# Cross attention on one core: from mixing the values with the attention to mixing x and applying the value weights behind it

## The chip, the core and the metric

The kernel runs on one core of a Trainium2 chip. The core has engines that work side by side, each through its own list in order: PE (matmuls, with PEld for the weight loads that overlap them), DVE (vector work), ACT (activations and copies), POOL (vector work on SBUF, and the issue of accumulating DMAs) and SP (here only issues DMAs). PE writes PSUM, eight banks of 512 columns; DVE and ACT read PSUM, POOL does not. The metric is the device time of one execution in microseconds.

## The reference

For each of 32 batches, with x and y of 256 channels x 1024 positions in fp32:

```python
x_q = jnp.einsum('oc,bcn->bno', w_qk, y)
x_k = jnp.einsum('oc,bcn->bon', w_qk, x)
x_v = jnp.einsum('oc,bcn->bon', w_v, x) + b_v[None, :, None]
energy = jnp.einsum('bnc,bcm->bnm', x_q, x_k)
attention = jax.nn.softmax(energy, axis=-1)
attention = attention / (1e-07 + attention.sum(axis=1, keepdims=True))
x_r = jnp.einsum('bcn,bnm->bcm', x_v, attention)
x_r = jax.nn.relu(jnp.einsum('oc,bcn->bon', w_t, x - x_r) + b_t[None, :, None])
return x + x_r
```

## The kernel before

Batches are worked through one after another, 1024 positions as eight row tiles n of 128, 256 channels as two halves. The weights are folded once at the start: `gw` is w_qk with itself, so that the energies are y times (gw x); `vw` is w_t times w_v; `tw` is w_t. Both folded ones carry a factor of 4096 (`UP`), which the next step takes out.

**Three forms.** Every operand of a large matmul is kept as three tiles, called HIGH, REST and LOW (`FORMS`), and every product is three matmuls, one for each form. Whoever makes an operand therefore makes three: a rounded copy (ACT), and two that come out of a difference and a sum (DVE from PSUM, POOL from SBUF, or an accumulating DMA that POOL issues).

**One batch.** Its matmuls, all of 128 x 128 weights, are:

- keys (k): `xf,gw`, 24 matmuls of 512 columns, into a pair of PSUM banks; ACT, DVE, DVE make the three forms `gf` of it.
- values (V): `vw,xf`, 48 matmuls of 256 columns: eight position tiles, each with x as the weights and `vw` as the moving operand, so that the result stands with positions on the partitions. ACT and DVE make its three forms, `uf`.
- straight (X): `xf,tw`, 24 of 512 columns; ACT adds the bias and puts it into `xe`.
- energies (E): `gf,yf`, for each row tile n 12 of 512 columns, into one of two pairs of banks that alternate. Then DVE takes the row minimum (`nm`), ACT the exponential with the row sum (`rs`), DVE its reciprocal (`ri`), ACT the HIGH form `ef` (two halves, h), DVE the REST form (r) and the column sums `acc` (sum), ACT a scaled copy (s), POOL the LOW form (l). When h, r and sum have read a half of the pair, the energies of tile n+2 may be written there.
- attention (A): `ef,uf`, for each n 12 of 512 columns, summed over all n into the last two pairs of banks, one pair for each half of the channels.

Behind the last A stands the end of the batch: DVE turns `acc` into the inverse column sums `rc` and divides (`z`), POOL adds `xe` (join), ACT takes the relu, POOL adds `xo`, which is x loaded a second time, and SP stores.

The queries y come by one load for the HIGH form and a second read of the same half batch that is accumulated onto the negated HIGH form, issued by POOL (`rest`, lines 176-177).

**The order.** `InOrder` (lines 55-69) ties every instruction of PE, DVE, ACT and POOL behind the last one written for that engine, so that the order of the code is the order of each engine; plain loads and stores on SP are placed by the framework that builds the program. The loop over batches (lines 605-752) writes the order by hand; the last batch has a table of words of its own, `STEPS` (lines 812-823), one word for each step, which stands in the code in one list for all engines.

Of the kernel before, what the change touches and what calls it, by code (L numbers as in the profile page):

```python
# [17 lines left out]
def kernel(  # L18
# [34 lines left out]
    sp = ctx.enter_context(tc.tile_pool(name="sp", bufs=4))  # L53
# [76 lines left out]
    xbias = const.tile([P, KC, 1], F32, name="xbias")  # L130
    for _ in range(5):
        pe.matmul(banks[:, 7, :P], zeros, zeros, start=True, stop=True)
    make_identity(nc, ident)

    work = one.tile([P, 4, KC * C], F32, tag="xe", name="work")

    def area(j):
        return work[:, j].rearrange("p (k c) -> p k c", k=KC)
# [22 lines left out]

    class Queries:

        def __init__(self, q):
            self.b, self.half = divmod(q, MH)
            self.from_ = raw(f"y_{self.b}_{self.half}").rearrange("p (k n) -> p k n", k=KC)
            load(self.from_, y_half(self.b, self.half))

        def high(self):
            self.f = yp.tile([P, FORMS, KC, MB], F32R, tag="yf", name=f"yf_{self.b}_{self.half}")  # L170
            act.copy(self.f[:, HIGH], self.from_)
# [32 lines left out]
    class Batch:  # L204

        def __init__(self, b):
            self.b = b
            self.at = b % 2
            self.row, self.ef, self.uf = {}, {}, []

        def load_x(self):
            self.xr = [raw_x("x", self.b, k) for k in range(KC)]
# [17 lines left out]
        def channels(self, p, w, i):  # L230

            for h in range(MH):
# [10 lines left out]
        def keys(self, i):  # L243
            if i == 0:
                self.gf = one.tile([P, FORMS, KC, N], F32R, tag="gf", name=f"gf_{self.b}")
            p = pair((self.at + i) % 2)
            self.channels(p, gw.forms, i)
            return Right(p, [self.gf[:, j, i] for j in range(FORMS)])

        def first_keys(self, j, k):  # L250
# [12 lines left out]
            return [Right(pair(i), [self.gf[:, f, i] for f in range(FORMS)]) for i in range(KC)]  # L263
# [17 lines left out]
        def straight(self, c, to=3):  # L281
            self.channels(pair(to), tw, c)
            self.x_from = pair(to)

        def straight_out(self, c, halves=None):
            if not hasattr(self, "xe"):
                self.xe = one.tile([P, KC, N], F32, tag="xe", name=f"xe_{self.b}")
            at = slice(0, MH) if halves is None else halves
            act.activation(
                self.xe[:, c].rearrange("p (h m) -> p h m", h=MH)[:, at],  # L290
                self.x_from[:, at],
                AF.Identity,
                bias=xbias[:, c],
                scale=1.0,
# [5 lines left out]
        def energy(self, n, halves=range(MH)):  # L300
            p = self.place(n)
            yf = ys[self.b * MH + n // HT].f
            for h in halves:
                for j in ORDER:
                    for k in range(KC):
                        matmul(
                            p[:, h],
                            yf[:, j, k, ts(n % HT, P)],
# [32 lines left out]
        def scaled(self, n):  # L341
            act.mul(self.ef[n][:, LOW], value(self.ef[n][:, HIGH]), 1.0 / UP)

        def low(self, n, at=slice(0, None)):
            f = self.ef[n][:, :, at]
            pool.tensor_tensor(f[:, LOW], value(f[:, LOW]), value(f[:, REST]), ALU.add)
# [44 lines left out]
        def inverse(self):  # L391
# [11 lines left out]
            self.turned()  # L403

        def turned(self):
# [11 lines left out]
        def divided(self, c):  # L417
            if c == 0:
                self.z = one.tile([P, KC, N], F32, tag="z", name=f"z_{self.b}")
            dve.scalar_tensor_tensor(  # L420
                self.z[:, c], flat(pair(2 + c)), ubias[:, c], self.rc, ALU.add, ALU.mult
            )

        def joined(self, c):
            pool.tensor_tensor(self.z[:, c], self.z[:, c], self.xe[:, c], ALU.add)

        def relu(self, c):
            act.activation(self.z[:, c], self.z[:, c], AF.Relu)
# [7 lines left out]

        def end_sum(self, c, at=slice(0, None)):
            xo = self.xo[c][:, at]
            pool.tensor_tensor(xo, xo, self.xe[:, c, at], ALU.add)

        def end_least(self, c, at=slice(0, None)):
            act.mul(self.xe[:, c, at], self.xe[:, c, at], -1.0)
# [23 lines left out]
        def piece(self, c, h):  # L466
# [3 lines left out]
            return pair(2 + c)[:, h], self.z[:, c, at], self.xe[:, c, at], self.xo[c][:, at]  # L470
# [74 lines left out]
    corner = work[:, 3, :P]  # L545
# [30 lines left out]
    def biases():  # L576
# [4 lines left out]
        for k in range(KC):  # L581
            act.activation(
                xbias[:, k], wtb[:, k : k + 1], AF.Identity, bias=bt[:, k], scale=-1.0
            )

    y0 = ys[0]
    y0.high()
    k0, k1 = cur.first_keys(LOW, 1)
    pool.tensor_tensor(y0.f[:, REST], y0.from_, value(y0.f[:, HIGH]), ALU.subtract)
    k1.high()  # L590
    k1.low()
    k0.high()
    k1.rest()
    k0.low()
    k0.rest()
    y0.scaled()
    pool.tensor_tensor(y0.f[:, LOW], value(y0.f[:, LOW]), value(y0.f[:, REST]), ALU.add)
    tw = const.tile([P, FORMS, KC, C], F32R, name="tw")
    th, tl, td = (tw[:, j].rearrange("p k c -> p (k c)") for j in range(FORMS))
    wd = work[:, 2]  # L600
    ys[2] = Queries(2)

    first_order = [(1, 0), (1, 1), (0, 0), (0, 1)]
    last = None
    for b in range(B - 1):
        nxt = Batch(b + 1)

        if b == 0:
            v0 = cur.values(0)
            v0.high()  # L610
            v1 = cur.values(1)
            v0.low()
            v0.rest()
            act.copy(th, wtT)
            pool.tensor_tensor(wd, wtT, value(th), ALU.subtract)
            pool.tensor_tensor(
                product, wt, bv.unsqueeze(1).to_broadcast([P, KC, C]), ALU.mult
            )
            ys[1].high()
            v1.high()  # L620
            act.mul(tl, wd, UP)
            pool.tensor_tensor(td, wtT, value(tl), ALU.subtract)
            cur.energy(0)
            cur.lowest(0)
            v1.low()
            ys[1].minus()
            ys[1].rest()
            biases()
            cur.exp(0)
            cur.energy(1)  # L630
            cur.recip(0)
            v1.rest()
            cur.forms(0)
            ys[1].scaled()
            ys[1].low()
            cur.lowest(1)
            cur.share(0)
            cur.straight(0)
            cur.exp(1)
            cur.straight_out(0)  # L640
            cur.recip(1)
            cur.straight(1, 2)
            for h in range(MH):
                cur.high(1, h)
                cur.rest(1, h)
            cur.straight_out(1)
            cur.scaled(1)
            cur.low(1)
        else:
            v0 = cur.values(0)  # L650
            v0.high()
            v1 = cur.values(1)
            v0.low()
            v0.rest()
            cur.energy(0)
            v1.high()
            v1.low()
            cur.lowest(0)
            v1.rest()
            cur.straight(0)  # L660
            cur.exp(0)
            cur.recip(0)
            cur.high(0, 0)
            cur.rest(0, 0)
            cur.high(0, 1)
            cur.rest(0, 1)
            cur.straight_out(0)
            cur.scaled(0)
            cur.low(0)
            cur.energy(1)  # L670
            cur.lowest(1)
            cur.share(0)
            cur.exp(1)
            cur.recip(1)
            cur.straight(1, 2)
            last.load_out()
            for h in range(MH):
                cur.high(1, h)
                cur.rest(1, h)
            cur.straight_out(1)  # L680
            cur.scaled(1)
            cur.low(1)
            last.relu(0)
            last.put(0)
        nxt.load_x()
        cur.energy(2)
        cur.share(1)
        for n in range(2, NT):
            if n > 2:
                cur.energy(n)  # L690
            cur.lowest(n)
            if n > 2:
                cur.share(n - 1)
            cur.exp(n)
            cur.recip(n)
            cur.forms(n)
            cur.attention(n - 2, first_order if n == 2 else None)
            if b == 0 and n == 4:
                gather_groups()
            if n == 2:  # L700
                nxt.x_high(0)
                nxt.x_rest(0)
            elif n == 3:
                nxt.x_high(1)
                nxt.x_rest(1)
                nxt.x_scaled(0)
            elif n == 4:
                nxt.x_scaled(1)
                nxt.x_low(0)
                nxt.x_low(1)  # L710
            if last and n == 5:
                last.relu(1)
                last.put(1)
            elif n == 5:
                ys[2].high()
                ys[2].minus()
                ys[2].rest()
            elif n == 6 and not last:
                ys[2].scaled()
                ys[2].low()  # L720
        k0 = nxt.keys(0)
        cur.share(NT - 1)
        k0.high()
        k0.low()
        k0.rest()
        cur.columns()
        cur.inverse()
# [129 lines left out]
```

## Time and profile before

| | |
|---|---|
| median of 3 runs | 1941.99 us (1941.97 to 1942.38) |
| the profiled execution | 1942.1 us, of which its span is 1940.3 us |
| granted clock of PE | 0.999 |
| PE busy | 1934.2 us, 9249 matmuls |
| DVE, ACT, POOL busy | 1558.5, 1463.5, 1261.3 us |
| DMA | 235.35 MB, 81852 packets |

The span is the time from the first to the last instruction of the profiled execution; the device time has 1.8 us more around it. PE counts as busy while a matmul is in flight, so neighbours overlap: the duration of one (389 ns) is its latency, and the rate is read from the distance of starts in the timeline. Almost every instruction stands under the one line of the helper that records them (line 66), so the groups are told apart by the names of their tiles. In a row `xf<-x` the tile on the left is written and the one on the right read.

### The profile page before, as it was taken

Reading aid. Unit: us, or ns where it says so; the run is one execution under the profiler, and the core shown is the slowest. Engines: PE = TensorE matmul, PEld = TensorE weight load, DVE = VectorE, ACT = ScalarE, POOL = GpSimd, SP = SyncE. Lnnn points to the kernel's source line nnn. Section 1 sums busy time; section 2 is a strip of 40 time slices with the busy share of each in tenths; the row PEclk is TensorE's granted clock in tenths of the full one; section 3 lists DMA queues with packets and bytes.
Section 4 is the critical chain, followed back from the end, with each engine's and each line's share of the span. In section 5 each row is a group of like instructions: output and inputs, shape, how many; then the busy total and the mean of one; then the engine's idle time right before and its main releaser. Section 6 shows DMA issues by size and latency. Waiting matters only on the chain.

```text
span 1940.3 us, 25180 instructions
## 1 busy us (share of the span) xinstructions
PE 1934.2 (100%) x9249; PEld 1632.4 (84%) x9249; DVE 1558.5 (80%) x2153; ACT 1463.5 (75%) x1874; POOL 1261.3 (65%) x654
## 2 busy tenths in 40 slices
PE   9999999999999999999999999999999999999998
PEld 8888888888888888888888888888888888888887
DVE  7887788877888778887788887888877888778888
ACT  7778777787777877778777778777777777877776
POOL 5576766667656676566766666665766657666566
PEclk9999999999999999999999999999999999999999
DMA  4654545545456444554445554545545455454541
GB/s 139 131 137 116 124 112 120 146 115 130 110 112 149 118 122 109 123 138 121 118 117 123 130 127 112 124 116 130 131 119 120 120 120 134 116 121 118 120 120 44
DMA packets 81852, 235.35 MB, mean 121 GB/s; under 512 B 7488, under 2 KB 8384, under 8 KB 81728
## 3 DMA queue, kind: packets, MB, share of 16 engines
q0 software_dynamic: 35136, 98.58, 29.1%
q1 hardware_dynamic: 46176, 134.76, 20.4%
q8 instruction: 73, 1.20, 0.3%
q14 instruction: 51, 0.42, 0.1%
q10 hardware_dynamic: 416, 0.39, 0.1%
HBM read 134.61 MB, written 33.55 MB: 87 GB/s over the span
## 4 chain that ended last, share of the span: by engine, by line
PE 100%; DMA 0%; DVE 0%; issue 0%
PE banks L66 100%; DMA stage<-in_L_xattn_w_qk_dram 0%; DVE banks L66 0%; DVE z L66 0%
## 5 line engine op out<-in xcount | busy, mean ns | idle before, releaser
L66 POOL TENSOR_TENSOR ef<-ef 128x1024 fp32r<-128x1024 f32 x253 | 608.9, 2407 | 450.2 <-ACT ef L66 443.3
L66 PE MATMUL banks<-gf,yf 128*128 128x512 f32 x3072 | 739.0, 389 | 0.0
L66 PE MATMUL banks<-ef,uf 128*128 128x512 f32 x3036 | 730.3, 389 | 0.0
L66 PEld LDWEIGHTS banks<-gf,yf 128*128 128x128 f32 x3072 | 574.5, 188 | 118.1 <-issue 0.3
L66 PEld LDWEIGHTS banks<-ef,uf 128*128 128x128 f32 x3036 | 569.9, 188 | 118.1
L66 DVE SCALAR_TENSOR_TENSOR ef<-banks,ri,ef 128x512 fp32r<-128x512 f32 x506 | 356.8, 747 | 204.2 <-ACT ef L66 204.2
L66 ACT ACTIVATE banks<-banks,nm 128x1024 f32<-128x1024 f32 x256 | 278.0, 1086 | 216.3 <-DVE nm L66 214.3
L66 DVE TENSOR_REDUCE nm<-banks 128x1 f32<-128x1024 f32 x256 | 313.0, 1222 | 86.5 <-PE banks L66 86.5
L66 ACT ACTIVATE ef<-banks,ri 128x512 fp32r<-128x512 f32 x506 | 320.7, 685 | 69.1 <-DVE ri L66 67.7
L66 DVE SCALAR_TENSOR_TENSOR acc<-banks,ri,acc 128x512 f32<-128x512 f32 x448 | 314.1, 743 | 0.2
L66 ACT ACTIVATE ef<-ef 128x1024 fp32r<-128x1024 f32 x253 | 268.9, 1063 | 5.9
L66 POOL DMA_DIRECT2D yf<-in_ctx_dram x63 | 77.1, 1223 | 188.7 <-ACT yf L66 186.6
L66 PEld LDWEIGHTS banks<-vw,xf 128*128 128x128 f32 x1536 | 188.7, 192 | 2.6
L66 PE MATMUL banks<-vw,xf 128*128 128x256 f32 x1536 | 189.5, 283 | 0.0
L66 PE MATMUL banks<-xf,gw 128*128 128x512 f32 x768 | 184.8, 389 | 0.0
L66 PE MATMUL banks<-xf,tw 128*128 128x512 f32 x768 | 184.3, 389 | 0.0
L66 PEld LDWEIGHTS banks<-xf,tw 128*128 128x128 f32 x768 | 144.2, 188 | 29.9
L66 PEld LDWEIGHTS banks<-xf,gw 128*128 128x128 f32 x768 | 144.1, 188 | 29.9
L66 POOL TENSOR_TENSOR z<-z,xe 128x1024 f32<-128x1024 f32 (+1 forms) x63 | 163.7, 2815 | 4.8 <-DVE z L66 4.8
L66 POOL TENSOR_TENSOR z<-z,xo 128x1024 f32<-128x1024 f32 (+1 forms) x65 | 152.9, 2353 | 0.2 <-DVE z L66 0.2
L66 POOL TENSOR_TENSOR xf<-x,xf 128x1024 fp32r<-128x1024 f32 x62 | 149.5, 2412 | 0.0
L66 ACT ACTIVATE yf<-yf 128x1024 fp32r<-128x1024 f32 x127 | 131.1, 1055 | 2.0
(89 smaller groups left out, 1336.8 us busy)
## 6 DMA issues: line engine op xcount, KB each, us to landing
x<-in_x_dram SPq DMA_DIRECT2D x64, 512.0 KB, 3.5
y<-in_ctx_dram SPq DMA_DIRECT2D x64, 512.0 KB, 4.6
xo<-in_x_dram SPq DMA_DIRECT2D x64, 512.0 KB, 3.6
yf<-in_ctx_dram POOLq DMA_DIRECT2D x63, 512.0 KB, 6.5
yf<-yf POOLq DMA_DIRECT2D x63, 512.0 KB, 5.3
xf<-xf POOLq DMA_DIRECT2D x62, 512.0 KB, 6.3
out_dram<-z SPq DMA_DIRECT2D x62, 512.0 KB, 2.9
out_dram<-z SPq DMA_DIRECT2D x4, 256.0 KB, 2.0
```

What stands on the lines that cost most here:

```text
L66: self.last = getattr(self.engine, name)(*args, **kwargs)
```

## The change

In all batches but the first and the last (`late(b)`) the order of the two products is turned round: the attention is applied to x itself, and `vw` to the result.

- The values matmuls go (48 of 256 columns). `uf` is now made from x with positions on the partitions. For that x is loaded another time, as 32-row groups (`load_positions`, eight DMAs of 128 KB to a batch, pieces of 512 bytes), DVE transposes it in place in blocks of 32 x 32 (`turned_x`, tt), and ACT and POOL make three forms of it: th (ACT copy), tm (POOL subtract), tl (ACT scale), tr (POOL add). `turned` reads the loaded tile in runs of 32 elements.
- The blocks bring the positions into another order, and the row tiles of y are formed in that order: `ordered` and `loaded` let the y steps write or read in runs of 32. REST of y is now a subtraction on POOL (yr) instead of the second, accumulated read.
- A sums the mixed x. Behind the last A three forms of it are made from PSUM: zh (ACT copy), zr and zl (DVE), for each half of the channels. Then `mixed` (W): `vw` as the weights, the mixed x as the moving operand, 24 matmuls of 512 columns. It writes the pair of the other half (`pair(3 - c)`), and the division reads that.
- The output: the addition of x on POOL with its load `xo` is replaced by an accumulating DMA from x into `z` (add), and the store is a step of its own (st).
- The two nested orders of before become three tables of words: `FIRST` (batches 0 and 1), `STEADY` (batches 2 to 30, one pass each) and a new `STEPS`. A leading `+` means the batch after, `-` the one before. E, X, k and W are now halves of 6 matmuls, A halves of 3, which other steps stand between.
- Pools: `xe` gets a pool of three buffers, one for each half of the channels; `sp` has three instead of four. The four buffers of raw loads now also hold the two tiles of turned x.

The places at the seam of two batches, as the two built programs have them (before: batches 10 and 11; `ef_11_0` is row tile 0 of batch 11). PE before:

```order
L66 MATMUL banks_76<-ef_10_6_5344,uf_10_1_5059 128x512 x12
L66 MATMUL banks_76<-xf_11_5195,gw_113 128x512 x12
L66 MATMUL banks_76<-ef_10_7_5383,uf_10_1_5059 128x512 x12
L66 MATMUL banks_76<-vw_148,xf_11_5195 128x256 x48
L66 MATMUL banks_76<-gf_11_5402,yf_11_0_4983 128x512 x12
L66 MATMUL banks_76<-xf_11_5195,tw_179 128x512 x12
L66 MATMUL banks_76<-gf_11_5402,yf_11_0_4983 128x512 x12
```

PE of the changed kernel at the same seam, up to the first two matmuls of W (`zf` is the mixed x):

```order
L67 MATMUL banks_79<-ef_10_6_5279,uf_10_1_4928 128x512 x9
L67 MATMUL banks_79<-ef_10_7_5305,uf_10_1_4928 128x512 x12
L67 MATMUL banks_79<-xf_11_5082,tw_176 128x512 x12
L67 MATMUL banks_79<-gf_11_5355,yf_11_0_4905 128x512 x24
L67 MATMUL banks_79<-zf_10_0_5400,vw_154 128x512
L67 MATMUL banks_79<-zf_10_1_5406,vw_154 128x512
```

The values are gone from the seam; between the last attention of batch 10 and the W that needs it stand half of the straight product and two row tiles of energies of batch 11, and behind the 24 matmuls of W come the other half, two more tiles of energies, and then the first attention of batch 11.

DVE of the changed kernel at that seam (`nm_11_0` is the row minimum of tile 0, `rc` the inverse column sums, `z` the division):

```order
L67 SCALAR_TENSOR_TENSOR gf_11_5355<-banks_79,gf_11_5355 128x1024
L67 TENSOR_TENSOR zf_10_0_5400<-banks_79,zf_10_0_5400 128x1024
L67 SCALAR_TENSOR_TENSOR zf_10_1_5406<-zf_10_1_5406,banks_79 128x1024
L67 SCALAR_TENSOR_TENSOR zf_10_0_5400<-zf_10_0_5400,banks_79 128x1024
L67 TENSOR_TENSOR zf_10_1_5406<-banks_79,zf_10_1_5406 128x1024
L67 TENSOR_REDUCE nm_11_0_5458<-banks_79 128x1
L67 STREAM_TRANSPOSE rc_10_5463<-sc_92 128x1024
L67 TENSOR_REDUCE nm_11_1_5465<-banks_79 128x1
L67 RECIPROCAL ri_11_0_5476<-rs_11_0_5461 128x1
L67 SCALAR_TENSOR_TENSOR z_10_5484<-banks_79,ubias_up_95,rc_10_5463 128x1024
L67 SCALAR_TENSOR_TENSOR ef_11_0_5479<-banks_79,ri_11_0_5476,ef_11_0_5479 128x512 x2
```

The four forms of the mixed x stand where the forms of the values stood, and the first division now stands in the middle of the first two row tiles of the next batch.

POOL before, at the seam:

```order
L66 TENSOR_TENSOR ef_10_7_5383<-ef_10_7_5383 128x1024
L66 DMA yf_11_1_5456<-in_ctx_2048_dram 128x2x512
L66 DMA yf_12_0_5464<-in_ctx_2048_dram 128x2x512
L66 TENSOR_TENSOR z_10_5481<-z_10_5481,xe_10_5100 128x1024 x2
L66 DMA yf_11_1_5456<-yf_11_1_5456 128x1024
L66 DMA yf_12_0_5464<-yf_12_0_5464 128x1024
L66 TENSOR_TENSOR ef_11_0_5576<-ef_11_0_5576 128x1024
```

and in the changed kernel:

```order
L67 TENSOR_TENSOR ef_10_7_5305<-ef_10_7_5305 128x1024
L67 DMA z_9_5010<-in_x_dram 128x1024
L67 TENSOR_TENSOR yf_11_1_5229<-y_11_1_5203,yf_11_1_5229 128x8x4x32
L67 DMA yf_11_1_5229<-yf_11_1_5229 128x1024
L67 TENSOR_TENSOR uf_11_1_5402<-xp_11_1_5208,uf_11_1_5402 128x1024
L67 TENSOR_TENSOR uf_11_0_5260<-xp_11_0_5108,uf_11_0_5260 128x1024
L67 TENSOR_TENSOR yf_12_0_5379<-y_12_0_5206,yf_12_0_5379 128x8x4x32
L67 DMA yf_12_0_5379<-yf_12_0_5379 128x1024
L67 TENSOR_TENSOR uf_11_1_5402<-xp_11_1_5208,uf_11_1_5402 128x1024
L67 TENSOR_TENSOR z_10_5484<-z_10_5484,xe_10_0_4948 128x1024
L67 TENSOR_TENSOR ef_11_0_5479<-ef_11_0_5479 128x1024
```

Five subtractions and additions in runs of 32 now stand between the last LOW form of one batch and the first of the next, and one join instead of two.

SP in the changed kernel, from the stores of batch 10 on:

```order
L539 DMA out_0_dram<-z_10_5484 128x1024
L114 DMA x_13_0_5982<-in_x_dram 128x1024
L539 DMA out_0_dram<-z_10_5484 128x1024
L114 DMA x_13_1_6008<-in_x_dram 128x1024
L265 DMA xp_13_0_6056<-in_x_dram 32x8x128 x4
L180 DMA y_13_1_6151<-in_ctx_2048_dram 128x2x512
L180 DMA y_14_0_6154<-in_ctx_2048_dram 128x2x512
L265 DMA xp_13_1_6156<-in_x_dram 32x8x128 x4
```

The second store of a batch now stands behind a load of x for a later batch, which waits until POOL has read the raw buffer that it takes; before, one store stood between the two loads of `xo` and the other behind the loads of x.

The diff, cut to its core:

```diff
+    xep = ctx.enter_context(tc.tile_pool(name="xep", bufs=3))
+    sp = ctx.enter_context(tc.tile_pool(name="sp", bufs=3))
...
+    def late(b):
+        return 0 < b < B - 1
...
+        def ordered(self, f):
+            if late(self.b):
+                return f.rearrange("p t k (g j) -> p (k g) t j", j=G32)
+            return f.rearrange("p t k n -> p k t n")
...
-        def minus(self):
-            act.mul(self.f[:, REST], value(self.f[:, HIGH]), -1.0)
         def rest(self):
-            accumulate(self.f[:, REST], y_half(self.b, self.half))
+            pool.tensor_tensor(
+                self.ordered(self.f[:, REST]),
+                self.loaded(),
+                self.ordered(value(self.f[:, HIGH])),
+                ALU.subtract,
+            )
...
+        def load_positions(self, q):
+            self.xp[q] = raw(f"xp_{self.b}_{q}")
+            to = self.xp[q].rearrange("p (c n) -> p c n", n=P)
+            from_ = x[self.b].rearrange("(c r) n -> r c n", r=G32)
+            for g in range(NG):
+                load(to[ts(g, G32)], from_[:, :, q * MB + g * P : q * MB + (g + 1) * P])
+        def turned_x(self, q):
+            blocks = self.xp[q].rearrange("p (j r) -> p j r", r=G32)
+            dve.transpose(blocks, blocks)
+        def turned(self, q):
+            return self.xp[q].rearrange("p (c t r) -> p t c r", t=HT, r=G32)
...
+        def turned_minus(self, q):
+            pool.tensor_tensor(
+                self.turned_form(q, LOW),
+                self.turned(q),
+                value(self.turned_form(q, HIGH)),
+                ALU.subtract,
+            )
...
+        def mixed_high(self, k):
+            f = ep.tile([P, FORMS, N], F32R, tag="ef", name=f"zf_{self.b}_{k}")
+            self.zf.append(f)
+            act.copy(f[:, HIGH], flat(pair(2 + k)))
+        def mixed_rest(self, k):
+            f = self.zf[k]
+            dve.tensor_tensor(f[:, REST], flat(pair(2 + k)), value(f[:, HIGH]), ALU.subtract)
...
+        def mixed(self, c, halves=range(MH)):
+            for h in halves:
+                for j in ORDER:
+                    for k in range(KC):
+                        matmul(
+                            pair(3 - c)[:, h],
+                            vw.forms[:, j, k, ts(c, P)],
+                            self.zf[k][:, j, ts(h, MB)],
+                            j == ORDER[0] and k == 0,
+                            j == ORDER[-1] and k == KC - 1,
+                        )
...
+        def added(self, c):
+            accumulate(self.z[:, c], x[self.b, ts(c, P)])
+        def stored(self, c):
+            load(out[self.b, ts(c, P)], self.z[:, c])
...
+    STEADY = """
+        X00 -zh0 th1 --st0 kr1 -zh1 yr1 -zr0 X01 E01 xw0 E00 -zl1 E10 -zl0 E11 -zr1 -W01
+        -W00 --st1 min0 +ys0 exp0 -turn min1 yl1 tm1 tr0 -W11 ri0 tl1 h00 h01 +yr0 +yl0
...
+    for b in range(2, B - 1):
+        for ahead, word in map(split, STEADY.split()):
+            do(word, b + ahead)
```

More of the change, by code (lines that the diff above doesn't have):

```diff
@@ L233, in channels @@
+        def channels(self, p, w, i, halves=range(MH)):
+            for h in halves:
                 for j in ORDER:
@@ L262, in first_keys @@
                     )
-            return [Right(pair(i), [self.gf[:, f, i] for f in range(FORMS)]) for i in range(KC)]
+                self.key_bank[i] = pair(i)
         def values(self, q):
@@ new lines, with at_batch, query, make @@
+    batches = {0: cur}
+    done = {("ldy0", 1)}
+    def at_batch(b):
+        if b not in batches:
+            batches[b] = Batch(b)
+        return batches[b]
+    def query(h):
+        def make(s):
+            ys[s.b * MH + h] = Queries(s.b * MH + h)
+        return make
+    def of_query(h, what):
+        return lambda s: getattr(ys[s.b * MH + h], what)()
+    def of_batch(what):
+        return lambda s, *a: getattr(s, what)(*a)
+    def half(what, *more):
+        return lambda s, c, h: getattr(s, what)(c, *more, [h])
```

438 lines of the change are left out of this document (224 added, 214 removed).

## The prediction

> **What bounds the kernel now.** I read the page first, for the load of each engine and for the chain that ended last.
>
> ```profile
> span 1940.3 us, 25180 instructions
> PE 1934.2 (100%) x9249; PEld 1632.4 (84%) x9249; DVE 1558.5 (80%) x2153; ACT 1463.5 (75%) x1874; POOL 1261.3 (65%) x654
> PE 100%; DMA 0%; DVE 0%; issue 0%
> ```
>
> PE is busy for all of the span but 6.1 us, and the chain is PE alone. "Busy" may hide slow issue, so the timeline of PE comes next, around the values of one batch, and then the windows view of the same batch.
>
> ```profile
> 914.29 2.88 PE L66 MATMUL banks<-ef,uf 128*128 128x512 f32 x12
> 917.01 5.92 PE L66 MATMUL banks<-vw,xf 128*128 128x256 f32 x48
> 922.76 2.91 PE L66 MATMUL banks<-gf,yf 128*128 128x512 f32 x12
> 925.51 2.88 PE L66 MATMUL banks<-xf,tw 128*128 128x512 f32 x12
> 928.23 2.88 PE L66 MATMUL banks<-gf,yf 128*128 128x512 f32 x12
> 917.01:977.15 60.14, 60.14 (x289) 50.82 (x288) 48.42 (x67) 45.58 (x59) 39.34 (x20) 1.00 0.51 123
> ```
>
> No row has idle time before it: twelve matmuls of 512 columns start 2.72 us ahead of what follows, whichever operands they have (227 ns each), and 48 of 256 columns take 922.76 - 917.01 = 5.75 us (120 ns each). A batch is 60.14 us, of which DVE (third number in the row of windows) is busy 48.42, ACT 45.58 and POOL 39.34. So any time taken from PE is gained and any wait put before PE is lost; the other engines cost nothing until PE waits for them.
>
> **The PE work removed.** Half the columns cost 120 of 227 ns, not half: a matmul has about 13 ns besides its columns. The 48 become 24 of 512 columns: 24 x 227 ns = 5.44 us. That is 5.75 - 5.44 = 0.31 us for each of 30 batches, 9.3 us in all. Nothing hides it, since PE is the chain. The Trainium skill, "TensorE: Matmul & The Clock Gate", section "Back-to-back issue gap", gives a gap of N/2.4 + 2.5 ns; an estimate from that page would be 48 x 109.2 - 24 x 215.8 = 62 ns a batch, 1.9 us in all and 1940.1 us. The trace's 227 and 120 ns disagree with it, and the rows decide.
>
> **Work that the other engines gain.** Their durations come from the groups, kept apart by shape:
>
> ```profile
> L66 POOL TENSOR_TENSOR ef<-ef 128x1024 fp32r<-128x1024 f32 x253 | 608.9, 2407 | 450.2 <-ACT ef L66 443.3 <-DVE ef L66 4.9
> L66 POOL TENSOR_TENSOR z<-z,xe 128x1024 f32<-128x1024 f32 x62 | 162.4, 2839 | 3.4 <-DVE z L66 3.4
> L66 POOL TENSOR_TENSOR xf<-x,xf 128x1024 fp32r<-128x1024 f32 x62 | 149.5, 2412 | 0.0
> L66 POOL TENSOR_TENSOR z<-z,xo 128x1024 f32<-128x1024 f32 x62 | 149.1, 2405 | 0.0
> L66 POOL DMA_DIRECT2D yf<-in_ctx_dram x63 | 77.1, 1223 | 188.7 <-ACT yf L66 186.6 <-issue 2.1
> L66 POOL DMA_DIRECT2D yf<-yf x63 | 68.5, 1091 | 15.2 <-DMA yf<-in_ctx_dram 5.8 <-issue 4.9 <-DVE acc L66 3.1
> L66 POOL TENSOR_TENSOR few<-few 128x32 f32<-128x32 f32 x1 | 0.3, 253 | 0.1
> L66 DVE SCALAR_TENSOR_TENSOR uf<-banks,uf 128x1024 fp32r<-128x1024 f32 x64 | 78.1, 1220 | 1.1
> L66 DVE SCALAR_TENSOR_TENSOR z<-banks,ubias,rc 128x1024 f32<-128x1024 f32 x62 | 79.3, 1279 | 6.0 <-DVE rc L66 6.0
> L66 DVE STREAM_TRANSPOSE rc<-sc 128x1024 f32<-128x1024 f32 x32 | 39.8, 1245 | 1.1
> L66 ACT ACTIVATE uf<-banks 128x1024 fp32r<-128x1024 f32 x64 | 65.7, 1027 | 79.0 <-PE banks L66 79.0
> L66 ACT CAST yf<-y 128x1024 fp32r<-128x1024 f32 x64 | 66.7, 1042 | 0.0
> L66 ACT ACTIVATE yf<-yf 128x1024 fp32r<-128x1024 f32 x127 | 131.1, 1055 | 2.0
> ```
>
> Per batch. DVE: zr and zl (four, 1.22 each) take the place of the four forms of the values at the same price; two transposes at 1.25 (row `rc<-sc`) come on top: 48.4 + 2.5 = 50.9 us. ACT: zh takes the place of HIGH of the values (1.03); th adds 2 x 1.04, tl 2 x 1.06, and the two negations of y (1.06) go: 47.7 us. POOL: yr, tm and tr are six operations, at 2.41 like `xf<-x,xf` 14.5 us; the two additions of `xo` (4.8 us) go; two issues of accumulating y reads (1.22) go and two accumulating x reads into `z` come: 39.3 + 9.7 = 49.0 us. PE's batch is 60.14 - 0.31 = 59.83 us, so the loads are 85%, 80% and 82%. No engine becomes the bound by its sum; what matters is whether each result comes in time.
>
> One price has no row: the six POOL operations step through runs of 32 elements. From below it is a plain row, 2.38 to 2.41 us. From above, each run as an instruction of its own (`few<-few`, 0.253 us for 32 elements): 32 x 0.253 = 8.1 us. I take 2.41, since the operand has the same number of elements and these stay adjacent in a run; I keep 2.84 (`z<-z,xe`, dearest of the plain ones) as an ordinary disturbance. For ACT's copies and DVE's transposes in place I take the plain rows for the same reason; from above the same doubling by short instructions would be needed to matter, see the spares below.
>
> **The seam in hand-made time.** The steps between engines are read from one row tile:
>
> ```profile
> 900.69 2.88 PE L66 MATMUL banks<-gf,yf 128*128 128x512 f32 x12
> 903.61 1.22 DVE L66 TENSOR_REDUCE nm<-banks 128x1 f32<-128x1024 f32 x1 [0.55 <-PE banks L66]
> 904.87 1.09 ACT L66 ACTIVATE banks<-banks,nm 128x1024 f32<-128x1024 f32 x1 [1.59 <-DVE nm L66]
> 906.10 0.17 DVE L66 RECIPROCAL ri<-rs 128x1 f32<-128x1 f32 x1
> 906.36 1.27 ACT L66 ACTIVATE ef<-banks,ri 128x512 fp32r<-128x512 f32 x2 [0.29 <-DVE ri L66]
> 907.08 1.41 DVE L66 SCALAR_TENSOR_TENSOR ef<-banks,ri,ef 128x512 fp32r<-128x512 f32 x2 [0.82 <-ACT ef L66]
> 907.66 1.06 ACT L66 ACTIVATE ef<-ef 128x1024 fp32r<-128x1024 f32 x1
> ```
>
> The next matmuls start at 903.41 and DVE at 903.61: 0.2 us from a slot's end to its reader; 0.04 from DVE to ACT, 0.1 around the reciprocal. Let 0 be the end of the last attention of a batch. PE then has X to 2.72, tiles 0 and 1 of the energies to 5.44 and 8.16, W to 13.60 (a half of the channels to 10.88), X to 16.32, tiles 2 and 3 to 19.04 and 21.76, then the first attention. Ready times against these slots:
>
> - W at 8.16. ACT: zh0 -0.5 to 0.6 (its half of the sums ended 0.68 earlier), th 1.5, zh1 2.4. DVE: zr0 to 1.8, zl1 2.5 to 3.7, zl0 4.9, zr1 6.0. Spare 2.1 us.
> - The first division (div0) starts at 10.88 + 0.2 = 11.1 and ends at 12.4; X behind W writes the same banks at 13.60. Spare 1.2. In DVE's list r of tile 0, the reciprocal, sum and r of tile 1 are behind it: sum of the half that tile 2 overwrites at 16.32 ends at 14.5, spare 1.8; r of tile 1 ends at 17.9 against 20.40.
> - The second division stands behind the minimum of tile 2: 19.24 + 1.22 + 1.28 = 21.7; attention writes those banks at 22.44. Spare 0.7, the smallest.
> - POOL: tm waits for th, 1.6 to 4.0; tr 6.4; yr 8.8; the yl issue (1.09) 9.9; tr 12.3; join (2.84, behind div0) 15.3; l of tile 0 17.7; l of tile 1 (behind its r) 20.4. The attention reads these as the last of three matmuls, at 22.2 and 24.25. Spare 3.8.
> - SP: the second store of the batch before stands behind the x load that waits for tr (6.4); it issues at 6.9.
>
> ```profile
> out_dram<-z SPq DMA_DIRECT2D x62, 512.0 KB, 2.9
> xf<-xf POOLq DMA_DIRECT2D x62, 512.0 KB, 6.3
> x<-in_x_dram SPq DMA_DIRECT2D x64, 512.0 KB, 3.5
> ```
>
> It lands at 9.8, and div0 writes the same tile `z`, so it must be there by 11.1; 1.3 us spare, and 1.2 more before X waits. The accumulating x read behind it (issued near -5, 6.3 to land) is there by 1.5. The turned x is loaded some 20 us ahead of its transposes, against 3.5 us for a plain load of the same bytes, so its small pieces may cost five times as much without a wait.
>
> In the middle of a batch the same sums give spares of 1.2 to 2.3 us (half of a tile's pair read before tile n+2, l before its attention). No wait of PE follows, the same as today. I cost the order of the steps at nothing, covered by these spares, and so also the two transposes (behind the minima of tiles 4 and 6, 1.4 us before DVE is late). The first batches, the last and the tail have new orders too, with PE work as before; without rows of their own I put them at 0, between -1.5 and +6 us (the part of the span without PE, once more).
>
> **Sum.** Span 1940.3 - 9.3 = 1931.0 us; the profiled execution took 1942.1, 0.1 above the median, so median 1941.99 - 9.3 = 1932.7 us.
>
> **Rivals.**
>
> 1. POOL's runs are dear. With d more for each operation, the four between th and tile 1 put the end of l at 20.0 + 4d, and PE begins to wait at d = 1.0; the gain is eaten at d = 1.1, that is 3.5 us an operation. At 3.6, a little beyond it, PE waits 0.64 us a batch: 30 x (0.64 - 0.31) = +10 us, 1952 us, and each further 0.1 us an operation costs 12 us more. For it: no row shows such an operand, and POOL's list is the one that grows most. Against: it needs 1.1 us where the largest spread among the plain rows is 0.43. The Trainium skill, "GPSIMD Engine Reference", section "Performance pitfalls for Q7 kernels", says that reads with a step of more than 8 bytes cost half as much again; inside a run the step here is 4 bytes, so by its letter it would not hold, and no run here shows it. Chance 0.11.
> 2. The store is late. Landing in 6.3 us, as the accumulating DMAs do, it puts div0 at 13.2 and X waits 1.0 us: 30 x (1.0 - 0.31) = +21, 1963 us; it decides from 5.6 us on. Against: the row has 2.9. Chance 0.05.
> 3. The one-off orders lose the 6 us: 1932.7 + 6 = 1938.7 us. Chance 0.10.
> 4. The 13 ns are no cost of each matmul: 48 halves of 227 ns would be 5.45 us, so there is no gain, 1942.0 us. Against: the 120 ns. Chance 0.02.
> 5. Other waits of more than 0.31 us a batch, at the spare of 0.7 above all, where DVE would have to come 2 us late to tile 2's minimum (it is free 1.3 us ahead): slower. Chance 0.04.
>
> **How the numbers follow.** What remains, 0.68, is the forecast, 1932.7 us; its own range is 1931 to 1937. A measurement of this kernel can tell about 0.2%, 3.9 us: faster is below 1938.1, slower above 1945.9. Faster 0.68 and half of rival 3, 0.73; same the other half and rival 4, 0.07; slower rivals 1, 2 and 5, 0.20. The range reaches from 1931 to 1950: it holds the forecast, rivals 3 and 4 and the lower half of rival 1, 0.86.
>
> **What the profile after would show.** Right: 9249 - 30 x 24 = 8529 matmuls; 2.72 us for every twelve through the seam, 5.44 for W, 59.83 us a batch; `uf<-xp` on POOL at 2.4 us; div0 waiting for PE, not for a DMA. Wrong: idle time before `ef,uf` with POOL named (1), idle time before `xf,tw` behind W (2), a loss that stands in the first or last 120 us alone (3). A wait of 0.31 us in each seam is enough to make it wrong.

## The result, and the profile after

| | before | after |
|---|---|---|
| median of six runs each, side by side | 1941.98 us (1941.76 to 1942.38) | 1933.86 us (1933.61 to 1936.91) |
| the profiled execution | 1942.1 us, span 1940.3 us | 1933.67 us, span 1931.7 us |
| first to last matmul start | 1933.92 us | 1923.45 us |
| last matmul start to the end of the span | 5.6 us | 7.5 us |

The changed kernel is faster by 8.1 us: the ratio is 0.996, with a 95% interval of 0.9947 to 0.9973. The forecast was 1932.7 us, 1.2 us lower. One of the six runs took 1936.91 us where the other five lie within 0.5 us; it is not explained.

The page of after, with the span, the busy time of each engine and the chain that ended last:

```profile
span 1931.7 us, 24665 instructions
PE 1923.8 (100%) x8529; PEld 1595.2 (83%) x8529; DVE 1622.3 (84%) x2213; ACT 1495.9 (77%) x1933; POOL 1531.7 (79%) x774
PE 100%; DVE 0%; issue 0%
```

The matmuls are 8529, and PE is still the chain. POOL's busy time went from 1261 to 1532 us and DVE's from 1559 to 1622 us, and none of it made PE wait. The seam of two batches shows that best. Here are the rows that matter from the timeline of after (start in us, duration, engine, instruction; idle time that the engine had before the row stands in brackets at its end, with what ended it), from the last attention of a batch, which ends at 906.58, to the first attention of the next:

```profile
906.10 1.02 ACT L67 CAST zf<-banks 128x1024 fp32r<-128x1024 f32 x1 [2.70 <-PE banks L67]
906.36 0.34 SPq L539 DMA_DIRECT2D out_dram<-z  x1
906.58 2.88 PE L67 MATMUL banks<-xf,tw 128*128 128x512 f32 x12
909.30 5.60 PE L67 MATMUL banks<-gf,yf 128*128 128x512 f32 x24
911.28 1.22 DVE L67 TENSOR_TENSOR zf<-banks,zf 128x1024 fp32r<-128x1024 f32 x1
912.95 0.33 SPq L114 DMA_DIRECT2D x<-in_x_dram  x1
914.74 5.60 PE L67 MATMUL banks<-zf,vw 128*128 128x512 f32 x24
917.66 1.28 DVE L67 SCALAR_TENSOR_TENSOR z<-banks,ubias_up,rc 128x1024 f32<-128x1024 f32 x1 [1.36 <-PE banks L67]
920.18 2.88 PE L67 MATMUL banks<-xf,tw 128*128 128x512 f32 x12
921.39 2.42 POOL L67 TENSOR_TENSOR ef<-ef 128x1024 fp32r<-128x1024 f32 x1
922.90 5.60 PE L67 MATMUL banks<-gf,yf 128*128 128x512 f32 x24
924.44 2.40 POOL L67 TENSOR_TENSOR ef<-ef 128x1024 fp32r<-128x1024 f32 x1 [0.64 <-ACT xe L67]
926.96 1.28 DVE L67 SCALAR_TENSOR_TENSOR z<-banks,ubias_up,rc 128x1024 f32<-128x1024 f32 x1
928.34 5.60 PE L67 MATMUL banks<-ef,uf 128*128 128x512 f32 x24
```

The rows of PE have no idle time before them. The product with `vw` takes 920.18 - 914.74 = 5.44 us, where the 48 narrow matmuls of before took 5.75. How much a batch gains is read over many. The windows view (length, then PE, PEld, DVE, ACT and POOL busy, granted clock, DMA share and GB/s) from one start of the product with `vw` to another, 28 batches on, is of before:

```profile
134.67:1819.73 1685.06, 1685.06 (x8066) 1422.67 (x8065) 1355.65 (x1876) 1277.21 (x1625) 1101.58 (x560) 1.00 0.51 123
```

and of after:

```profile
136.82:1812.34 1675.52, 1675.52 (x7393) 1387.85 (x7392) 1416.67 (x1933) 1311.10 (x1682) 1351.86 (x673) 1.00 0.50 124
```

A batch takes 1685.06 / 28 = 60.18 us before and 1675.52 / 28 = 59.84 after, and PE is busy for all of both. 0.34 us a batch are 10.2 us in 30 batches. The product itself saves 0.31 of the 0.34; the starts in the trace show the other 0.03 in the twelve matmuls that come right behind the narrow ones, which take 2.747 us before and 2.720 after.

The engines that were given more work had these prices in the groups of after (busy us, mean ns of one, then idle time before them and what ended it), and the view of the tile `xp` gives lowest, median and highest of the operation on runs of 32:

```profile
L67 POOL TENSOR_TENSOR uf<-xp,uf 128x1024 fp32r<-128x1024 f32 x120 | 296.4, 2478 | 82.0 <-ACT uf L67 81.9
L67 POOL TENSOR_TENSOR yf<-y,yf 128x1024 fp32r<-128x1024 f32 x64 | 168.0, 2626 | 11.6 <-ACT yf L67 11.6
L67 POOL TENSOR_TENSOR z<-z,xe 128x1024 f32<-128x1024 f32 x62 | 150.5, 2427 | 3.2
L67 DVE SCALAR_TENSOR_TENSOR z<-banks,ubias_up,rc 128x1024 f32<-128x1024 f32 x60 | 76.8, 1279 | 39.0 <-PE banks L67 39.0
L67 DVE STREAM_TRANSPOSE xp<-xp 128x1024 f32<-128x1024 f32 x60 | 74.0, 1234 | 0.0
L67 DVE TENSOR_TENSOR zf<-banks,zf 128x1024 fp32r<-128x1024 f32 x60 | 73.2, 1222 | 25.9 <-ACT zf L67 25.9
L67 PE MATMUL banks<-zf,vw 128*128 128x512 f32 x720 | 168.2, 389 | 0.0
```

```profile
L67 POOL TENSOR_TENSOR uf<-xp,uf x120: 2391/2402/2726, 66.3 to 1813.8; 128x1024 fp32r<-128x1024 f32 x120
```

The runs of 32 cost POOL nothing in the median: 2402 ns, beside 2409 ns of the plain `xf<-x,xf` before. The mean of 2478 comes from 30 of the 120, all at the same place in their batch, that took about 2.7 us. The transposes in place cost 1.23 us and the forms of the mixed x 1.22, as plain rows of the same size did. The first division waits for PE and not for a DMA.

Two things went the other way. One is in the DMA issues of the page (count, KB each, us from issue to landing):

```profile
out_dram<-z SPq DMA_DIRECT2D x62, 512.0 KB, 5.9
x<-in_x_dram SPq DMA_DIRECT2D x64, 512.0 KB, 4.0
xp<-in_x_dram SPq DMA_DIRECT2D x240, 128.0 KB, 2.7
z<-in_x_dram POOLq DMA_DIRECT2D x60, 512.0 KB, 5.3
```

A store needs 5.9 us to land in the median, where it needed 2.9; no wait of PE came of it, and why is told below. The other is the tail. From first to last matmul the kernel is 10.5 us shorter (10.2 in the batches, the rest in waits of PE in the first 21 us, which differ from trace to trace), but 1.9 us were given back behind the last one: its distance to the end of the span went from 5.6 to 7.5 us. The timelines of both kernels have the same work there. Before:

```profile
1932.91 3.75 POOL L66 TENSOR_TENSOR z<-z,xo 128x512 f32<-128x512 f32 x3 [0.17 <-DVE z L66]
1934.23 3.48 SPq L496 DMA_DIRECT2D out_dram<-z  x4
1936.66 0.69 DVE L66 TENSOR_TENSOR z<-banks,xo 128x512 f32<-128x512 f32 x1
```

After:

```profile
1922.83 3.75 POOL L67 TENSOR_TENSOR z<-z,xo 128x512 f32<-128x512 f32 x3
1924.15 3.26 SPq L611 DMA_DIRECT2D out_dram<-z  x4
1926.19 0.69 DVE L67 TENSOR_TENSOR z<-banks,xo 128x512 f32<-128x512 f32 x1
```

The last addition on DVE ends 2.95 us before the end of before's span and 4.8 us before the end of after's. What stands between is in the trace's records of the engines' closing instructions, which the timeline view leaves out. SP's waits for the stores of after were over at 1929.6 us, 2.1 us before the end, so the stores did not set it. POOL closes its list with a drain, which stands in the records as one instruction:

```
          POOL's last addition ends    its drain               drain ends behind the addition
before    1936.67                      1934.62 to 1939.25      2.6 us
after     1926.58                      1924.18 to 1930.96      4.4 us
```

So the span of after ends with POOL's drain, and that runs 1.8 us longer behind the last addition than before. The addition itself ends 0.4 us later, counted from the start of the last matmul (2.35 us behind it instead of 1.96). Against these 2.2 us stand 0.3 us that before waited for its stores: SP's last wait there was over at 1939.5, just behind the drain. That makes the 1.9 us. With a drain as short as before, the stores would set the end of after, and by the same records (4.80 us from the last matmul to SP's last wait before, 5.36 after) I estimate that 0.6 of the 1.9 us would remain.

### The profile page after: what moved, and what is told of

Read it like the earlier page. It is cut to its first block, busy times and chain, and to the rows that moved or that the text cites. A ratio compares the mean times of both kernels' runs of the same rounds, so it can differ in the third digit from the quotient of the medians.

```text
span 1931.7 us, 24665 instructions
## 1 busy us (share of the span) xinstructions
PE 1923.8 (100%) x8529; PEld 1595.2 (83%) x8529; DVE 1622.3 (84%) x2213; ACT 1495.9 (77%) x1933; POOL 1531.7 (79%) x774
## 2 busy tenths in 40 slices
DMA packets 129996, 233.73 MB, mean 121 GB/s; under 512 B 10320, under 2 KB 72656, under 8 KB 129872
## 4 chain that ended last, share of the span: by engine, by line
PE 100%; DVE 0%; issue 0%
PE banks L67 100%; DVE banks L67 0%; DVE z L67 0%
## 5 line engine op out<-in xcount | busy, mean ns | idle before, releaser
L67 POOL TENSOR_TENSOR ef<-ef 128x1024 fp32r<-128x1024 f32 x253 | 617.3, 2447 | 263.7 <-ACT ef L67 219.2
L67 PE MATMUL banks<-gf,yf 128*128 128x512 f32 x3072 | 728.3, 389 | 0.0
L67 DVE SCALAR_TENSOR_TENSOR ef<-banks,ri,ef 128x512 fp32r<-128x512 f32 x506 | 370.6, 743 | 17.5 <-ACT ef L67 16.1
L67 POOL TENSOR_TENSOR uf<-xp,uf 128x1024 fp32r<-128x1024 f32 x120 | 296.4, 2478 | 82.0 <-ACT uf L67 81.9
L67 DVE SCALAR_TENSOR_TENSOR acc<-banks,ri,acc 128x512 f32<-128x512 f32 x448 | 327.8, 744 | 5.4 <-ACT share L67 0.3
L67 POOL TENSOR_TENSOR yf<-y,yf 128x1024 fp32r<-128x1024 f32 x64 | 168.0, 2626 | 11.6 <-ACT yf L67 11.6
L67 PE MATMUL banks<-zf,vw 128*128 128x512 f32 x720 | 168.2, 389 | 0.0
L67 PEld LDWEIGHTS banks<-zf,vw 128*128 128x128 f32 x720 | 135.2, 188 | 28.0
L67 POOL TENSOR_TENSOR z<-z,xe 128x1024 f32<-128x1024 f32 (+1 forms) x63 | 151.8, 2409 | 5.1 <-DVE z L67 1.9
L67 ACT CAST zf<-banks 128x1024 fp32r<-128x1024 f32 x60 | 60.9, 1016 | 80.2 <-PE banks L67 80.2
```

The source lines that it names most:

```text
L67: self.last = getattr(self.engine, name)(*args, **kwargs)
```

## The experiments

The theory was: PE alone sets the time, the gain is what 24 matmuls of 512 columns save over 48 of 256, and all the work that moved to DVE, ACT and POOL lies inside spare times that are small but enough. The rivals were that the gain comes from the new order, that PE is close to being held up by another engine, and that POOL, whose work grew most, is what limits the kernel.

### The product behind the attention in narrow matmuls

`w_narrow` undoes the one part that should give the gain: the order, the loads, POOL's and DVE's work stay, and each product of 512 columns becomes two of 256.

```diff
-                for j in ORDER:
-                    for k in range(KC):
-                        matmul(pair(3 - c)[:, h], vw.forms[:, j, k, ts(c, P)],
-                               self.zf[k][:, j, ts(h, MB)], ...)
+                for t in range(2):
+                    for j in ORDER:
+                        for k in range(KC):
+                            matmul(pair(3 - c)[:, h, ts(t, C)], vw.forms[:, j, k, ts(c, P)],
+                                   self.zf[k][:, j, ts(2 * h + t, C)], ...)
```

> The changed kernel with its 24 matmuls of W (512 columns) cut into 48 of 256, in the same place and order, with the same columns and results. Theory (each matmul costs about 13 ns besides its columns, and PE is the chain): 30 x 0.31 = 9.3 us come back, 1933.9 + 9.3 = 1943.2 us, with twelve matmuls of 512 columns still 2.72 us apart and the 48 at 5.75 us. Rival (the gain came from the new order of the steps, not from the number of matmuls): no change, 1934 us.

It took 1943.95 us (1943.76 to 1944.9), a ratio of 1.001 to before, with an interval of 1.0001 to 1.002. The timeline of PE at the seam:

```profile
919.34 5.92 PE L67 MATMUL banks<-zf,vw 128*128 128x256 f32 x48
925.09 2.91 PE L67 MATMUL banks<-xf,tw 128*128 128x512 f32 x12
```

The product takes 5.75 us again, and all of the gain is gone, 10.1 us, as the 10.2 of the windows have it. The theory holds, and the rival, by which the order would keep the gain, falls. The run tells one thing more. From first to last matmul this kernel needs 1933.85 us and before 1933.92, yet it takes 1.9 us more: that is the price of everything in the change that is not the width of the product. Its last matmul starts at 1934.63 and its span ends at 1942.1, so the 1.9 us stand behind the last matmul, as in after.

### One third of the product left out

`w_two_forms` leaves out the LOW form in the product with `vw`: 8 of 24 matmuls in each of 30 batches, 240 in all. The three forms are still made.

```diff
-                for j in ORDER:
+                for j in (HIGH, REST):
...
```

> The changed kernel without the LOW pass of W, 8 of its 24 matmuls, so that the product is made of two forms alone. Theory (PE is still the bound, and by the spares nothing else waits within 1.8 us): 30 x 8 x 226.7 ns = 54.4 us less, 1879.5 us. Rival (the other engines have taken up their room, DVE at 84% and POOL at 79%): PE begins to wait in the seam, and less than 40 us is gained, 1894 us or more.

It took 1879.91 us (1879.45 to 1880.67), a ratio of 0.9681 with an interval of 0.9667 to 0.9696. Its page:

```profile
span 1877.7 us, 24185 instructions
PE 1869.3 (100%) x8289; PEld 1549.4 (83%) x8289; DVE 1621.4 (86%) x2213; ACT 1488.5 (79%) x1933; POOL 1526.8 (81%) x774
```

That is 53.95 us less than after, and 240 matmuls of 227 ns are 54.5. PE can be made 1.8 us a batch shorter and still sets the time: no other engine becomes the bound within that, though the spare times are short. How much further it would go was not tested.

### More work for POOL

The step that makes REST of the turned x is issued again behind the first join, once in `pool_plus_one` and twice in `pool_plus_two`. It writes the same values again, and takes the place of a run-of-32 price that is too high.

```diff
+        "again": lambda s, i: s.turned_rest(1),
...
-        ... E21 -join0 r10
+        ... E21 -join0 again0 again1 r10
```

> The changed kernel with the last addition of turned x (uf<-xp on POOL, 2.4 us) issued a second time in 29 batches, behind the first join and ahead of the LOW form of tile 0; the second writes the same values. Theory: in the seam at 906.58 us of the changed kernel POOL ends the LOW form of tile 1 at 926.84 and PE's first reader of it starts at 928.34 + 11 x 0.227 = 930.8, a spare of about 3.9 us, so 2.4 us cost nothing: 1934 us. Rival (POOL's list is already what PE waits for): 29 x 2.4 = +70 us, 2004 us; or half of that.

> The same with the addition issued twice more, 4.8 us. Theory: 4.82 - 3.9 = 0.9 us of waiting in each of 29 batches, +27 us, 1961 us, as idle time of PE before ef,uf of tile 1 with POOL named, and nowhere else. This is the price of runs of 32 that rival 1 of the prediction would have had at 1.2 us for each of four operations. Rival (other work on PE or a later idle time of POOL takes it up): under 1940 us; or (the late LOW form also makes the tiles behind it late): over 1975 us.

With one more, 2.4 us a batch, the time was 1933.66 us (1933.21 to 1934.76), ratio 0.9958, interval 0.9944 to 0.9973: nothing, as expected. With two it was 1947.35 us (1947.02 to 1947.86), ratio 1.0027, interval 1.0016 to 1.0038. So PE does begin to wait between the two, where the theory had put it, but the price is half of that forecast: 13.5 us in place of 27. The view of waits (idle us in total, times, longest us) and rows of the timeline at the seam that starts at 912.28:

```profile
PEld banks L67 <- POOL ef L67: 20.6, 58, 1.9
```

```profile
927.09 4.90 POOL L67 TENSOR_TENSOR uf<-xp,uf 128x1024 fp32r<-128x1024 f32 x2
931.95 4.76 POOL L67 TENSOR_TENSOR ef<-ef 128x1024 fp32r<-128x1024 f32 x2
934.04 6.01 PE L67 MATMUL banks<-ef,uf 128*128 128x512 f32 x24
```

The first attention spreads over 6.01 us, where the same 24 matmuls took 5.60 in after: the wait is inside it. From one product with `vw` to the next, a batch takes 60.23 us instead of 59.84 in 27 of the 29, which is 0.39 us more; the two others lose 0.9 and 2.1 us, the second in a seam where POOL stood idle for 2.3 us for a reason that the trace does not show. The expectation had taken 4.8 us of work against a spare of 3.9. It left out that POOL itself idled in after, in the row that starts at 924.44 above: 0.64 us before the LOW form of tile 1, waiting for ACT. A longer list of POOL fills that first: in `pool_plus_one` the idle time is gone, and here the two additions move the end of that LOW form by 4.2 us, from 20.26 us behind the last attention to 24.43 (936.71 - 912.28). Its reader, the twelfth matmul of the attention, would have started at 934.04 + 11 x 0.227 = 936.54 and starts at 936.77, 0.23 us late. The rest of the 0.39 us is small gaps, most of them right behind that matmul. One more thing the expectation had excluded: the 58 waits are two in each batch, since the weight load for tile 0 waits for its LOW form too, though outside the two dearer batches hardly any time is lost there.

### More work for DVE, at the smallest spare

The prediction gave the second division 0.7 us, the smallest spare. `dve_plus_one` makes the turned inverse sums again between the row minimum of tile 2 and that division, 1.25 us more.

```diff
+        def inverse_turned_again(self):
+            dve.transpose(self.rc.rearrange("p (j r) -> p j r", r=G32), sc.to_broadcast([P, NB, G32]))
...
-        ... +xh0 +xs0 A011 min2 -div1
+        ... +xh0 +xs0 A011 min2 -turnagain -div1
```

> The changed kernel with the transpose that makes rc (DVE, 1.24 us) made a second time in 29 batches, between the minimum of tile 2 and the second division; it writes the same values. Theory (the second division is the step with the smallest spare): in the seam at 906.58 us that division ends at 928.24 and the attention that overwrites its banks starts at 929.02, 0.7 us to spare with the step between engines; the transpose moves it 1.14 us, so PE waits about 0.46 us in each of 29 batches, +13 us, 1947 us, as idle time in the first matmuls of ef,uf. Rival (DVE's idle time of 1.5 us ahead of that minimum gives it room, or the steps behind are moved too): under 1936 us, or over 1955 us.

It took 1953.65 us (1953.36 to 1954.06), ratio 1.0058, interval 1.0043 to 1.0074: 19.8 us more than after, where 13 were expected. Waits and rows of the timeline:

```profile
PEld banks L67 <- DVE z L67: 23.5, 29, 0.8
PE banks L67 <- DVE z L67: 11.3, 29, 0.4
```

```profile
936.15 1.23 DVE L67 STREAM_TRANSPOSE rc<-sc 128x1024 f32<-128x1024 f32 x1
937.42 1.28 DVE L67 SCALAR_TENSOR_TENSOR z<-banks,ubias_up,rc 128x1024 f32<-128x1024 f32 x1
937.53 0.84 PE L67 MATMUL banks<-ef,uf 128*128 128x512 f32 x3
938.75 5.05 PE L67 MATMUL banks<-ef,uf 128*128 128x512 f32 x21 [0.39 <-DVE z L67]
```

The attention runs three matmuls and then stands, since the division still reads the banks that the fourth writes. At three times 227 ns the fourth would have started at 938.21; it starts at 938.75, 0.05 us behind the division's end at 938.70, so it is 0.55 us late. The 1.25 us put in less 0.55 is a spare of 0.7, as predicted. The matmuls behind it do not run at their rate at once, though. The distances of starts sum to about 0.13 us more a batch, 0.11 of it in the one gap behind the late matmul; that makes 0.68 us, and 29 times that is 19.7. The weight loads stand too while PE waits (the first of the two rows of waits), and I take the extra gaps to be the loads that had no matmul to run beside. That is a guess: no run separates it.

### The tail

`tail_dve` gives one of POOL's last three additions to DVE and lets POOL end earlier, to see whether the drain follows.

```diff
-            if c == h == 1:
-                dve.tensor_tensor(zh, p, xh, ALU.add)
+            if h == 1:
+                dve.tensor_tensor(zh, p if c else zh, xh, ALU.add)
...
-        ... A700 d00 A710 el1 d10 m10 A601 A701 d01 m01
-        plus A511 A611 A711 d11 o10 m11 relu o00 o01 o11
+        ... A700 d00 A710 el1 d10 m10 plus o10 A601 A701 d01 m01
+        o01 A511 A611 A711 d11 m11 relu o00 o11
```

> The changed kernel with one of the three last additions of POOL (128 x 512, 1.3 us) given to DVE, into a gap of 0.5 us ahead of the last division, and the two others in the same order. In the changed kernel POOL's last drain ends 4.4 us behind its last addition, at 1930.96 of 1931.7 us, while the last store is known to have landed at 1929.5; before it was 2.6 us behind, and inside the time of the stores. Theory (the drain follows POOL's last addition, and the end of the program waits for it): the span loses 1.2 us, 1932.6 us; PE's work does not move. Rival (the drain lasts until something else is over, or the stores or the division take its place): no change, 1933.9 us.

It took 1933.40 us (1933.26 to 1933.72), ratio 0.9955, interval 0.9942 to 0.9967. The drain did follow: POOL's last addition ended at 1925.38 us, 1.2 earlier, and the drain ran to 1929.76, again 4.4 us behind it. But SP's last wait now ended at 1930.4 us where it was 1929.6, and the span came out at 1931.2. So 0.5 us of the 1.2 came through and the stores took the drain's place. This is the fastest of the kernels that do all the work, but 0.46 us from after is less than this measurement can tell. Why the drain stands 4.4 us behind POOL's last addition in all kernels with the new order and 2.6 in the old one, no run settles; the additions themselves take the same 3.75 us in before and after.

## Why the prediction was right, point by point

- **The PE work removed: right.** Predicted were 0.31 us a batch and 9.3 in all; the product went from 5.75 to 5.44 us, the batch from 60.18 to 59.84, and undoing the width alone costs 10.1 us. The term was 0.9 us too small, because the 0.03 us in the matmuls behind the narrow ones were not seen. They stood in the rows of the prediction: the twelve from 922.76 to 925.51 take 2.75 us, not 2.72 like the others. The 60.14 us hid them, since the ends of that window had been set by hand; the next narrow matmuls of before start at 977.19 and not at 977.15, and the mean over 28 batches is 60.18. The 13 ns besides the columns are a cost of each matmul, and rival 4 falls. The estimate from the Trainium skill, "TensorE: Matmul & The Clock Gate", section "Back-to-back issue gap", 1940.1 us, falls with it: 24 matmuls more cost 5.75 - 5.44 us, which is 13 ns each and not 2.5. That section gives its formula for an isolated matmul, which the prediction left out when it used it for a stream of them.
- **Prices on the other engines: right.** DVE was to be 50.9 us a batch, ACT 47.7 and POOL 49.0; the window of 28 batches has 1416.67 / 28 = 50.6, 46.8 and 48.3. The runs of 32 cost 2.402 us, the value taken out of 2.38 to 8.1, so rival 1 did not come about. The point from which POOL's four operations would have made PE wait was put a little low, at 1.0 us dearer each. It stood on 20.0 us for the end of POOL's list, with the join at 2.84 us; the join took 2.41 (row `z<-z,xe`), so the list ends at 19.6 by itself, and 24.25 - 19.6 = 4.6 us of room are about 1.15 for each of four. `pool_plus_two` agrees: 4.86 us more, and the reader 0.23 us late. The 0.64 us of waiting that rival 1 has at 3.6 us an operation come out at about 0.5 from its own 20.0 + 4d and 24.25; no verdict hangs on it.
- **The spares at the seam: right where they were tested.** The last form of the mixed x was put at 6.0 us behind the last attention and ended at 5.9 (912.50 - 906.58). The first division was to start at 11.1 and did at 11.08. The second was to end at 21.7 and ended at 21.66, with the spare of 0.7 that `dve_plus_one` confirmed. The LOW forms of tiles 0 and 1 were put at 17.7 and 20.4 and ended at 17.2 and 20.3.
- **SP and the store: wrong in its mechanism, without a price.** The prediction let the second store stand behind an x load that waits for tr, issue at 6.9 us and land in 2.9. The timeline of after, just ahead of the seam, has the load in front of the store:

```profile
901.50 2.89 POOL L67 TENSOR_TENSOR yf<-y,yf 128x1024 fp32r<-128x1024 f32 x1
904.42 0.35 SPq L114 DMA_DIRECT2D x<-in_x_dram  x1
```

It goes out 0.03 us behind an earlier step of POOL, yr, and the store follows at 906.36, 0.2 us before the seam's zero; the load that goes out at 912.95, when tr has ended, stands behind the store. What the store itself waits for is the accumulating read of x into `z`: SP's waits name it for 60 of the 62 stores of this line. The landing then took 5.9 us in the median and 7.3 us for this store, and not 2.9. By the prediction's own sum a store at 6.9 that lands in 5.9 us or more would have made the first division late; it was not late, since the issue was 7 us earlier than worked out, and the store was there 7.1 us behind the zero, 4 us ahead of the division. That no wait came of it is luck: two misses met. Rival 2 had asked for a landing of 5.6 us or more, which came about; it cost nothing because its issue time was wrong.
- **The one-off orders: the term that was mis-sized.** They were put at 0, between -1.5 and +6. `w_narrow` measured them: 1.9 us, with the matmuls from first to last as long as before. They stand behind the last matmul, where POOL's last addition ends 0.4 us later and its drain 1.8 us later still, less 0.3 us for which before had waited for its stores. In the orders of the first batches and the last the trace has no wait of PE longer than 0.1 us, beyond those for the first weights, which before has too. This is rival 3 in kind, at a third of its size.
- **The sum.** -10.2 of PE and +1.9 of the tail give -8.3 us; the medians differ by -8.1. The forecast of -9.3 came near since the two misses, 0.9 and 1.9 us, have opposite signs; the mechanism was right, and that the number is within 1.2 us is in part luck.

## What to carry to other kernels

Where one engine is the chain, its list alone gives the sum, and a large rebuild around it is worth exactly what it takes off that list; half as many matmuls of twice the width saved 13 ns for each one that went and a little behind them, here 10.2 us for 270 us more POOL work. The rest of the working should go into the spare time of each result at its reader, written out for one seam in order of time, since 2.4 us more on one engine were free and 1.25 on another cost 20. Write the last few microseconds behind the last matmul out in the same way: they gave back a fifth of the gain.

## What the runs showed of the chip that was not expected

- A wait of PE cost more than its own length in the two runs that made it wait: 0.55 us of waiting cost 0.68 us in `dve_plus_one`, and 0.23 us cost 0.39 us in `pool_plus_two`, mostly in gaps behind it.
- Stores of 512 KB took 5.9 us in the median to land instead of 2.9, with the mean DMA rate at 121 GB/s in both kernels; the packets grew from 81852 to 129996, and the 61440 pieces of 512 bytes of the turned x are more than the whole increase. That these are the cause was not tested.
- POOL's drain at the end of the program runs from 1924.18 to 1930.96 us in after, beside and beyond its last additions, and it can be what the span ends with when all stores have landed.
- POOL's price for the same addition moved with its place, not with its operand: `z<-z,xe` went from 2839 to 2427 ns in the mean, and `yf<-y,yf`, with the same shapes everywhere, takes 2.4 us at one place of a batch and 2.9 at the other. The reason was not tested.
